# One-hot places by one comparison for eight token tiles, in both routed stages of a gated cross-attention kernel

## The chip, the cores and the metric

The kernel runs on one core of one Trainium2 chip. The metric is the device time of one launch in microseconds (us). A core has TensorE (PE, the matmuls; PEld are its weight loads), VectorE (DVE), ScalarE (ACT), GpSimd (POOL) and SyncE (SP), and DMA queues issued from several of them.

## The reference, cut to what matters

Four layers of cross-attention, each followed by a feed-forward part, work on 16 x 128 = 2048 tokens of width 256. Layers 0 and 2 have a mixture of experts as their feed-forward part (MoE 0 and MoE 2 below): a router gives each token two of eight experts, and every token also passes through a shared expert.

```python
logits = x @ gate_w.T
scores = jax.nn.softmax(logits, axis=-1)
topk_w, topk_idx = jax.lax.top_k(scores, K)          # K = 2 of E = 8
...
y_sel = y_all[topk_idx, tok]                          # y_all: silu(x w1) * (x w3) @ w2, of each expert
y = jnp.sum(y_sel * topk_w[..., None], axis=1)
shared = jax.nn.silu(x @ sw1) * (x @ sw3) @ sw2
return (y + shared).reshape(hidden_states.shape)
```

## The kernel before, in words

The tokens lie in SBUF as 16 tiles of 128 partitions (B = 16, P = 128). In a routed stage the kernel computes no expert for tokens that did not choose it. It sorts the 4096 pairs of token and expert into blocks of 128 rows, each block of a single expert: at most NBLK = 40 blocks. `spots` finds the position `ps` of each pair in that order, and splits it into a block `blk` (0 to 39) and a place `at` within the block (0 to 127). Then it builds the inverse, `who`: which token stands in each place of each block. POOL gathers the normalised tokens by `who` with indirect DMAs (`load`, L593 in MoE 0 and L848 in MoE 2, two for each pair of blocks), and the experts' matmuls run over the blocks.

The inverse is a product of one-hot matrices, summed over 32 tiles of pairs (2 choices x 16 token tiles). For tile q the matrix `inp[:, q]` (128 x 128) has a nonzero element where a token's place equals the column's number, and `inb[:, q]` (128 x 40) a one where its block equals the column's number; TensorE adds `inp[:, q].T @ inb[:, q]` into `w` (L436, 32 matmuls), so that `w[place, block]` is the token's number. Before the change the number stands in `inp`: each of 32 instructions (L431) compares the row `slot` (0 to 127) with the tile's place and multiplies by the tile's token numbers, both per-partition scalars. `inb` comes from one comparison of 1280 elements (L421). `inp` is made in four tiles of eight, from three buffers shared under the tag `xn`; the fourth waits until the first has been read by TensorE. Both are written as fp32r, fp32 bits for TensorE's faster pass.

`spots` is a generator, run by `route` in `stage_moe0` and `stage_moe2`. The order of PE, DVE and ACT instructions is written out by hand (`manual_schedule`): between its yields the stage puts pieces of the shared expert (`fill`), so that TensorE has work while DVE routes. After the tile n of `inp` is made, the stage yields; before tiles 0 and 2 of the matmuls it places a `fill`:

```python
for n in range(4):
    next(r)
    if n % 2 == 0:
        fill()
next(r, None)
```

So TensorE's order is: shared expert, matmuls of `inp` 0 and 1, shared expert, matmuls of `inp` 2 and 3, and then the shared expert's rest while the gathers run. While DVE is busy with routing, the shared expert uses ACT and POOL in place of DVE. In MoE 0 a piece goes TensorE `up` (L477), ACT `sil` (L485, L490), POOL `hid` (L491), TensorE `th` (L497), ACT `hT` (L499), TensorE `y` (L505), ACT `ysh` (L511), POOL addition to `x` (L512). In MoE 2 it goes TensorE `ub` (L875), ACT `sil` and `gcopy` (L883, L889), POOL `hid` (L890), TensorE `tg` (L897), ACT `hT` and `hcopy` (L902, L904), POOL `hT` (L905), TensorE `yb` (L913), ACT `ysh` (L940), POOL addition to `x` (L941). After `who` (L437) the pieces use DVE again. The program holds the four layers a second time for inputs that need another softmax; that half does not run here.

Of the kernel before, what the change touches and what calls it, by code (L numbers as in the profile page):

```python
# [10 lines left out]
F32 = mybir.dt.float32  # L11
# [3 lines left out]
ALU = mybir.AluOpType  # L15
# [3 lines left out]
P = 128  # L19
B = 16  # L20
# [11 lines left out]
NBLK = 40  # L32
# [23 lines left out]
def passage(ctx: ExitStack, tc: tile.TileContext, a: dict, out: bass.AP, inv, flag):  # L56
    nc = tc.nc
# [108 lines left out]
    def bc(ap, axis, n):  # L166

        u = ap.unsqueeze(axis)
        shape = list(u.shape)
        shape[axis] = n  # L170
        return u.to_broadcast(shape)
# [170 lines left out]
    def sorter(pool):  # L342

        I32 = mybir.dt.int32
        c = {}
        upper = pool.tile([P, P], BF16, name="upper")
        nc.gpsimd.memset(upper, 1.0)
        nc.gpsimd.affine_select(
            out=upper, in_=upper, pattern=[[1, P]], compare_op=ALU.is_gt, fill=0.0, base=0, channel_multiplier=-1
        )  # L350
        onesb = pool.tile([P, P], BF16, name="onesb")
        nc.gpsimd.memset(onesb, 1.0)
        c["upper"], c["onesb"] = upper, onesb

        def counting(name, n, step, by_row):
            t = pool.tile([P, n], I32, name=f"{name}i")
            nc.gpsimd.iota(t, pattern=[[step, n]], base=0, channel_multiplier=by_row)
            c[name] = pool.tile([P, n], F32, name=name)
            nc.gpsimd.tensor_copy(c[name], t)

        counting("token", B, P, 1)
        counting("block", NBLK, 1, 0)
        counting("slot", P, 1, 0)

        for name, shape in (("ct", [P, E, B]), ("ce", [P, B, E])):
            c[name] = pool.tile(shape, F32, name=name)
            nc.gpsimd.memset(c[name], 1.0)
            nc.gpsimd.memset(c[name][:, :, 0:1], 0.0)
        return c
# [17 lines left out]
    def spots(mr, mo, psa, cn, one, pos, who, offs, inb):  # L387

        f, g = "p t e -> p (t e)", "p e t -> p (e t)"
        mb = mr.tile([P, B, E], BF16, name="mb")  # L390
        nc.vector.tensor_tensor(mb, one[:, 0], one[:, 1], ALU.add)
        yield
        pc = psa.tile([P, 2, B, E], F32, name="pc", tag="a")
        for i, w in enumerate((cn["upper"], cn["onesb"])):
            nc.tensor.matmul(pc[:, i].rearrange(f), lhsT=w, rhs=mb.rearrange(f), start=True, stop=True)
        cnt = mr.tile([P, E, B], F32, name="cnt")
        nc.vector.tensor_copy(cnt, pc[:, 1].rearrange("p t e -> p e t"))
        run = mr.tile([P, E, B], F32, name="run")
        nc.vector.tensor_tensor_scan(run.rearrange(g), cn["ct"].rearrange(g), cnt.rearrange(g), 0.0, ALU.mult, ALU.add)
        nb = mr.tile([P, E], F32, name="nb")  # L400
        nc.vector.tensor_scalar(nb, run[:, :, B - 1], 1.0 / P, 0.49609375, ALU.mult, ALU.add)
        nc.vector.tensor_scalar(nb, nb, MAGIC, None, ALU.add)
        nc.vector.tensor_scalar(nb, nb, MAGIC, None, ALU.subtract)
        be = mr.tile([P, E], F32, name="be")
        nc.vector.tensor_tensor_scan(be, ones[:, 0:E], nb, 0.0, ALU.mult, ALU.add)
        nc.vector.tensor_tensor(nb, be, nb, ALU.subtract)
        nc.vector.tensor_tensor(run, run, cnt, ALU.subtract)
        nc.vector.scalar_tensor_tensor(run, bc(nb, 2, B), float(P), run, ALU.mult, ALU.add)
        at = mr.tile([P, B, E], F32, name="at")
        nc.vector.tensor_tensor(at, pc[:, 0], run.rearrange("p e t -> p t e"), ALU.add)  # L410
        ps = mr.tile([P, 2, B], F32, name="ps")
        nc.vector.tensor_tensor(one, one, bc(at, 1, 2), ALU.mult)
        nc.vector.tensor_reduce(ps, one, AX.X, ALU.add)

        blk = mr.tile([P, 2, B], F32, name="blk")
        nc.vector.tensor_scalar(blk, ps, 1.0 / P, -0.49609375, ALU.mult, ALU.add)
        nc.vector.tensor_scalar(blk, blk, MAGIC, None, ALU.add)
        nc.vector.tensor_scalar(blk, blk, MAGIC, None, ALU.subtract)
        at = mr.tile([P, 2, B], F32, name="place")
        nc.vector.scalar_tensor_tensor(at, blk, -float(P), ps, ALU.mult, ALU.add)  # L420
        nc.vector.tensor_tensor(  # L421
            inb, bc(blk.rearrange("p i t -> p (i t)"), 2, NBLK), bc(cn["block"], 1, 2 * B), ALU.is_equal
        )
        yield

        w = psa.tile([P, NBLK], F32, name="w", tag="a")
        for q in range(0, 2 * B, 8):
            inp = mo.tile([P, 8, P], F32R, name="inp", tag="xn", bufs=3)
            for n in range(8):
                i, t = divmod(q + n, B)  # L430
                nc.vector.tensor_scalar(  # L431
                    inp[:, n], cn["slot"], at[:, i, t : t + 1], cn["token"][:, t : t + 1], ALU.is_equal, ALU.mult
                )
            yield
            for n in range(8):
                nc.tensor.matmul(w, lhsT=inp[:, n], rhs=inb[:, q + n], start=(q + n == 0), stop=(q + n == 2 * B - 1))  # L436
        nc.vector.tensor_scalar(who, w, B * P - 1.0, None, ALU.min)  # L437
        nc.vector.tensor_copy(pos, ps)

        le = mr.tile([1, NBLK, E], F32, name="le")  # L440
        jf = mr.tile([1, NBLK], F32, name="jf")
        nc.vector.tensor_tensor(le, bc(be[0:1], 1, NBLK), bc(cn["block"][0:1], 2, E), ALU.is_le)
        nc.vector.tensor_reduce(jf, le, AX.X, ALU.add)
        nc.vector.tensor_scalar(jf, jf, E - 1.0, float(WE), ALU.min, ALU.mult)
        nc.vector.tensor_copy(offs, jf)
# [12 lines left out]
    def stage_moe0(we, s13, s2, gw, tgc, sh, pos, wgt, cn, xs, ys, work):  # L458
# [63 lines left out]
        with tc.tile_pool(name="mr", bufs=1) as mr, tc.tile_pool(name="mo", bufs=2) as mo, tc.tile_pool(  # L522
# [48 lines left out]
            def route():  # L571

                t3 = lambda n: mr.tile([P, B, E], F32, name=n)
                l, ex = t3("l"), t3("ex")
                nc.vector.tensor_copy(l, lg)
                mx = mr.tile([P, 2, B], F32, name="mx")
                nc.vector.tensor_reduce(mx[:, 0], l, AX.X, ALU.max)
                nc.vector.tensor_tensor(ex, l, bc(mx[:, 0], 2, E), ALU.subtract)
                nc.scalar.activation(ex, ex, AF.Exp)
                one = first_two(mr, cn, ex, mx, -2.0)  # L580
                yield from spots(mr, mo, psa, cn, one, pos, who, offs, inb)
                s = mr.tile([P, B], F32, name="s")
                nc.vector.tensor_tensor(s, mx[:, 0], mx[:, 1], ALU.add)
                nc.vector.reciprocal(s, s)
                nc.vector.tensor_scalar(s, s, tg[:, tgc : tgc + 1], None, ALU.mult)
                nc.vector.tensor_tensor(wgt, mx, bc(s, 1, 2), ALU.mult)
# [152 lines left out]
    def stage_moe2(kv1, we, gw, gb, tgc, pos, wgt, cn, xs, ys):  # L739
# [4 lines left out]
        with tc.tile_pool(name="mr", bufs=1) as mr, tc.tile_pool(name="mo", bufs=2) as mo, tc.tile_pool(  # L744
# [60 lines left out]
            def route():  # L805
# [33 lines left out]
                nc.vector.tensor_reduce(wgt, gate, AX.X, ALU.add)  # L839
                nc.vector.tensor_scalar(wgt, wgt, tg[:, tgc : tgc + 1], None, ALU.mult)  # L840
                yield from spots(mr, mo, psa, cn, one, pos, who, offs, inb)

            xbs, xbTs, regs, hids, hTs = {}, {}, {}, {}, {}
# [1095 lines left out]
    with tc.tile_pool(name="kv1", bufs=1) as kv1:  # L1939
# [6 lines left out]
        cn = sorter(kv1)  # L1946
# [118 lines left out]
```

## Time and profile before

| | |
|---|---|
| median of 4 runs | 1064.28 us (1062.79 to 1065.0) |
| the profiled execution, its own time | 1062.89 us |
| its span, first to last instruction | 1061.1 us |
| mean granted TensorE clock | 0.912 |
| DVE busy | 609.7 us (57%) |
| POOL busy | 341.5 us (32%) |
| L431, one-hots of places | 64 instructions, median 336 ns, longest 2242 ns |
| L421, one-hots of blocks | 2 instructions of 1280 elements, 1482 ns |
| L436, their product | 64 matmuls, median 266 ns |
| `spots` in MoE 0, L421 to `who` | 177.4 to 196.5 us |
| `spots` in MoE 2, L421 to `who` | 635.3 to 654.8 us |

All times inside the program count from the start of the span. A row of the timeline has start, length, engine, line, operation, written and read tiles, count, and in brackets the idle time of the engine before it and what ended it. A row of the groups has the shapes, the count, the busy time, the mean in ns, and the idle time before. "Granted clock" is the share of TensorE's full clock that the chip gave; in this trace it is 1.0 or 0.5, and it changes at steps of a grid of 3.41 us.

### The profile page before, as it was taken

Reading aid. Unit: us, or ns where it says so; the run is one execution under the profiler, and the core shown is the slowest. Engines: PE = TensorE matmul, PEld = TensorE weight load, DVE = VectorE, ACT = ScalarE, POOL = GpSimd, SP = SyncE. Lnnn points to the kernel's source line nnn. Section 1 sums busy time; section 2 is a strip of 40 time slices with the busy share of each in tenths; the row PEclk is TensorE's granted clock in tenths of the full one; section 3 lists DMA queues with packets and bytes.
Section 4 is the critical chain, followed back from the end, with each engine's and each line's share of the span. In section 5 each row is a group of like instructions: output and inputs, shape, how many; then the busy total and the mean of one; then the engine's idle time right before and its main releaser. Section 6 shows DMA issues by size and latency. Waiting matters only on the chain. (4 is left out here: it accounts for less than half of the span.)

```text
span 1061.1 us, 14892 instructions
## 1 busy us (share of the span) xinstructions
PE 897.7 (85%) x5212; PEld 597.2 (56%) x5212; DVE 609.7 (57%) x1537; ACT 457.6 (43%) x707; POOL 341.5 (32%) x389
## 2 busy tenths in 40 slices
PE   2899978999999987888865758898179999998796
PEld 1444456777778544455443657887145555555564
DVE  5988866322224566777688678544445565434342
ACT  1211023233322446676763243455268888881111
POOL 5765422544105324311011126650533433101000
PEclk9999988999999988999996558999569999998899
DMA  9100070133332107900000202452588887610000
GB/s 305 45 1 0 1 210 34 55 104 110 80 119 71 42 24 108 117 1 1 1 1 0 80 0 65 145 141 82 147 249 248 231 221 217 166 41 1 21 31 33
DMA packets 71401, 94.12 MB, mean 89 GB/s; under 512 B 9271, under 2 KB 63127, under 8 KB 69015
## 3 DMA queue, kind: packets, MB, share of 16 engines
q1 hardware_dynamic: 56952, 67.21, 21.5%
q0 software_dynamic: 14080, 23.78, 11.4%
q10 hardware_dynamic: 288, 2.10, 0.5%
q8 instruction: 45, 0.74, 0.3%
q14 instruction: 36, 0.29, 0.1%
HBM read 57.06 MB, written 33.55 MB: 85 GB/s over the span
## 5 line engine op out<-in xcount | busy, mean ns | idle before, releaser
L1667 ACT ACTIVATE pt<-s 128x1024 f32<-128x1024 f32 x128 | 127.4, 1024 | 25.9 <-PE s L1660 22.1
L709 POOL DMA_INDIRECT yc<-ys,pos x64 | 62.3, 973 | 124.3 <-DVE x L729 48.8
L297 PE MATMUL y<-kv,toep 128*128 128x512 f32 x192 | 86.7, 603 | 1.1 <-DVE toep L237 1.1
L289 POOL TENSOR_TENSOR kv<-ctxT 128x1024 f32<-128x1024 f32 x32 | 60.2, 1899 | 28.5 <-PE y L297 28.5
L1676 PE MATMUL av<-pt,v 128*32 128x256 f32 x1024 | 69.2, 388 | 0.1
L1660 PE MATMUL s<-qa,ka 64*128 64x256 f32 x512 | 64.7, 334 | 3.4 <-ACT pt L1667 2.7
L1660 PEld LDWEIGHTS s<-qa,ka 64*128 64x128 f32 x512 | 38.8, 188 | 41.3 <-issue 18.2
L297 PEld LDWEIGHTS y<-kv,toep 128*128 128x128 f32 x192 | 35.6, 192 | 43.2 <-issue 39.8
L1687 DVE COPY avs<-av 128x256 f32<-128x256 f32 x64 | 27.1, 423 | 55.8 <-PE av L1676 55.8
L593 POOL DMA_INDIRECT xb<-xs,who x40 | 38.1, 952 | 41.1 <-PE tb L605 33.0
L616 PE MATMUL ub<-L0we,xbT 128*128 x160 | 50.7, 460 | 0.2 <-ACT xbT L607 0.2
L913 PE MATMUL yb<-L2we,hT 88*128 (+1 forms) x224 | 41.5, 312 | 7.8 <-DVE hT L737 5.0
L302 DVE TENSOR_TENSOR pr<-y,qT 128x1024 f32<-128x1024 f32 x32 | 39.0, 1222 | 12.3 <-PE y L297 9.4
L848 POOL DMA_INDIRECT xb<-xs,who x40 | 38.0, 950 | 22.9 <-PE tb L860 14.0
L1567 POOL TENSOR_TENSOR hl<-f,hl 128x512 fp32r<-128x512 f32 x16 | 20.5, 1281 | 74.3 <-ACT hl L1566 74.3
L477 PE MATMUL up<-L0s,xT 128*128 128x352 f32 x128 | 43.2, 483 | 0.0
L913 PEld LDWEIGHTS yb<-L2we,hT 88*128 88x128 f32 x224 | 33.1, 201 | 14.9 <-DVE hT L737 10.7
L1086 PE MATMUL s<-qa,ka 18*128 18x512 f32 x128 | 36.5, 647 | 4.2 <-ACT follow L1380 4.2
L305 DVE TENSOR_REDUCE oT<-pr 128x128 f32<-128x1024 f32 x32 | 38.9, 1219 | 1.0
L1676 PEld LDWEIGHTS av<-pt,v 128*32 128x32 f32 x1024 | 26.9, 110 | 20.4 <-issue 0.7
L642 PE MATMUL yb<-L0we,hTb 88*128 x160 | 37.9, 379 | 0.0
L1089 ACT ACTIVATE pt<-s 128x1024 f32<-128x1024 f32 x32 | 32.3, 1023 | 10.3 <-PE s L1086 10.1
(384 smaller groups left out, 2028.2 us busy)
## 6 DMA issues: line engine op xcount, KB each, us to landing
scr<-hl SPq DMA_DIRECT2D x64, 256.0 KB, 3.2
ys<-ysb SPq DMA_DIRECT2D x40, 256.0 KB, 2.1
qa<-scr SPq DMA_DIRECT2D x32, 256.0 KB, 4.3
ka<-scr SPq DMA_DIRECT2D x32, 256.0 KB, 5.3
L2we<-in_L_w_dram POOLq DMA_DIRECT2D x6, 792.0 KB, 6.5
L0we<-in_L_w_dram SPq DMA_DIRECT2D x6, 704.0 KB, 7.5
xs<-xn SPq DMA_DIRECT2D x8, 512.0 KB, 4.0
ctxT<-in_ctxT_dram ACTq DMA_DIRECT2D x2, 1024.0 KB, 5.9
```

The costliest lines, as they stand in the source:

```text
L289: nc.gpsimd.tensor_tensor(t, bc(ch, 3, 8), bc(ch, 2, 8), ALU.mult)
L297: nc.tensor.matmul(y[:, ns], lhsT=T[:, h, d : d + P], rhs=kv[mc][:, ns], start=(mc == 0), stop=(mc == lc))
L302: nc.vector.tensor_tensor(pr, y.rearrange("p (b j i) -> p b j i", b=B, j=8), bc(qT[:, lc, :, hs], 2, 8), ALU.mult)
L305: nc.vector.tensor_reduce(oT[:, lc, :, hs], pr, AX.X, ALU.add)
L477: nc.tensor.matmul(t[:, n, 0 : 2 * I], lhsT=xT[:, c, b * P : (b + 1) * P], rhs=s13[:, c, n, :], start=(c == 0), stop=(c == 1),)
L593: nc.gpsimd.indirect_dma_start(out=xbs[s][:, i, :], out_offset=None, in_=xs, in_offset=bass.IndirectOffsetOnAxis(ap=who[:, 2 * s + i : 2 * ...
L616: nc.tensor.matmul(t[:, i, 0 : 2 * I], lhsT=xbT[:, i, c, :], rhs=we[:, bass.ds(regs[s][i] + c * 2 * I, 2 * I)], start=(c == 0), stop=(c == 1),
L709: nc.gpsimd.indirect_dma_start(out=got[b][:, i, :], out_offset=None, in_=ys, in_offset=bass.IndirectOffsetOnAxis(ap=pos[:, i, b : b + 1], ...
L913: nc.tensor.matmul(y[:, i, :], lhsT=hT[:, x, k, i, :], rhs=we[0:HI, bass.ds(at[i] + 4 * I + k * D, D)], start=(n == 0), stop=(n == 3),)
L1660: nc.tensor.matmul(s[:, h, jj, :], lhsT=ka[r, 2 * i + jj, sc * P : (sc + 1) * P], rhs=qa[r, 2 * i + jj, :], start=True, stop=True,)
L1667: nc.scalar.activation(pts[b, i][:, sc], s, AF.Exp)
L1676: nc.tensor.matmul(av[c : c + 32, :], lhsT=va[:, sc, 8 * h + 2 * i + jj, :], rhs=pt[:, sc, h, jj, :], start=(sc == 0), stop=(sc == 1),)
```

## The change

One-hots of eight token tiles are written by one comparison of 1024 elements, in which the places are broadcast along the columns and `slot` along the tiles. A comparison of that form cannot multiply by the token's number as well, so the number goes into the block rows: after L421, two instructions of 640 elements each multiply `inb` in place, one for each choice. `inp` then holds ones and `inb` token numbers; their product is the same `w`. In each routed stage 32 instructions become 4, and 2 are new. In the new file the products are L426, the comparison L433 and the matmuls L438.

```diff
         nc.vector.tensor_tensor(
             inb, bc(blk.rearrange("p i t -> p (i t)"), 2, NBLK), bc(cn["block"], 1, 2 * B), ALU.is_equal
         )
+        for i in range(2):
+            u = inb[:, i * B : (i + 1) * B]
+            nc.vector.tensor_tensor(u, u.bitcast(F32), bc(cn["token"], 2, NBLK), ALU.mult)
         yield
 
         w = psa.tile([P, NBLK], F32, name="w", tag="a")
         for q in range(0, 2 * B, 8):
             inp = mo.tile([P, 8, P], F32R, name="inp", tag="xn", bufs=3)
-            for n in range(8):
-                i, t = divmod(q + n, B)
-                nc.vector.tensor_scalar(
-                    inp[:, n], cn["slot"], at[:, i, t : t + 1], cn["token"][:, t : t + 1], ALU.is_equal, ALU.mult
-                )
+            i, t = divmod(q, B)
+            nc.vector.tensor_tensor(inp, bc(at[:, i, t : t + 8], 2, P), bc(cn["slot"], 1, 8), ALU.is_equal)
             yield
             for n in range(8):
                 nc.tensor.matmul(w, lhsT=inp[:, n], rhs=inb[:, q + n], start=(q + n == 0), stop=(q + n == 2 * B - 1))
```

`bc(ap, axis, n)` repeats a tile's values n times along a new axis, by a stride of zero.

## The prediction

> **What bounds the kernel now.** I read the page first, for the shares and the clock; then the timeline of both stretches in which `spots` runs; then the windows cut at the steps of the clock; last the waits of the second stretch and the groups by shape, for prices.
>
> ```profile
> PE 897.7 (85%) x5212; PEld 597.2 (56%) x5212; DVE 609.7 (57%) x1537; ACT 457.6 (43%) x707; POOL 341.5 (32%) x389
> ```
>
> TensorE is the busiest engine, and DVE work alone is worth nothing unless TensorE waits for it. The chain of waits reaches back to 739 us only, behind both routed stages, so I judge each stretch by its own timeline. In the first stage (MoE 0):
>
> ```profile
> 177.36 1.48 DVE L421 TENSOR_TENSOR inb<-blk,block 128x1280 fp32r<-128x1280 f32 x1
> 178.76 8.66 DVE L431 TENSOR_SCALAR inp<-slot,place,token 128x128 fp32r<-128x128 f32 x24
> ...
> 179.84 0.96 POOL L491 TENSOR_TENSOR hid<-sil 128x352 f32<-128x352 f32 x1 [3.14 <-issue]
> ...
> 180.85 0.55 PE L497 MATMUL th<-ident,hid 128*128 128x128 f32 x3 [0.75 <-POOL hid L491]
> ...
> 188.36 2.12 PE L436 MATMUL w<-inb,inp 128*128 128x40 f32 x16
> ...
> 189.63 2.75 DVE L431 TENSOR_SCALAR inp<-slot,place,token 128x128 fp32r<-128x128 f32 x8 [2.21 <-PE w L436]
> ...
> 196.30 0.20 DVE L437 TENSOR_SCALAR who<-w 128x40 uint32<-128x40 f32 x1 [3.92 <-PE w L436]
> ```
>
> The 24 one-hots end at 187.42, before TensorE reaches L436 at 188.36 behind the shared expert's matmuls; the last 8 end at 192.38, and TensorE takes them at 194.14. TensorE waits for POOL (`hid`, L491), never for `inp`. The second stage (MoE 2) is different:
>
> ```profile
> 635.30 1.48 DVE L421 TENSOR_TENSOR inb<-blk,block 128x1280 fp32r<-128x1280 f32 x1
> 635.31 2.26 POOL L890 TENSOR_TENSOR hid<-gcopy,sil 128x352 f32<-128x352 f32 x1 [0.62 <-ACT gcopy L889]
> ...
> 636.70 16.85 DVE L431 TENSOR_SCALAR inp<-slot,place,token 128x128 fp32r<-128x128 f32 x32
> ...
> 639.44 1.34 POOL L905 TENSOR_TENSOR hT<-hcopy,hT 88x512 fp32r<-88x512 f32 x1 [0.64 <-ACT hcopy L904]
> ...
> 646.39 1.42 PE L436 MATMUL w<-inb,inp 128*128 128x40 f32 x5 [1.60 <-DVE inp L431]
> ```
> ```profile
> 639.02:642.44 3.42, 2.25 (x18) 2.00 (x17) 3.42 (x7) 1.55 (x4) 2.24 (x2) 1.00 0.00 0
> 642.44:645.85 3.41, 2.35 (x19) 2.25 (x17) 3.41 (x4) 2.04 (x5) 3.05 (x3) 1.00 0.00 0
> 645.85:649.26 3.41, 2.87 (x12) 2.87 (x13) 3.41 (x13) 0.00 (x0) 0.40 (x1) 0.50 0.00 0
> 649.26:652.68 3.42, 3.42 (x15) 3.37 (x14) 3.42 (x8) 1.75 (x3) 2.11 (x2) 0.50 0.00 0
> 652.68:656.09 3.41, 3.41 (x31) 3.41 (x31) 2.30 (x7) 0.82 (x3) 2.47 (x3) 1.00 0.00 0
> ```
>
> Columns: length, busy time of PE, PEld, DVE, ACT, POOL, granted clock, DMA. Here TensorE waits 1.60 us for `inp`, and the clock is halved from 645.85 to 652.68: 2.87 + 3.42 = 6.3 us of work, about 3.1 us of it owed to the clock.
>
> **Durations.** One comparison repeats each 0.256 us (1.60 us for four, less one of 0.336, over three at 186 us), so eight cost 2.05 us undisturbed, and 32 cost 8.2 us per stage. For a `tensor_tensor` with both operands in SBUF there are two undisturbed rows:
>
> ```profile
> L421 DVE TENSOR_TENSOR inb<-blk,block 128x1280 fp32r<-128x1280 f32 x2 | 3.0, 1482 | 0.0
> L838 DVE TENSOR_TENSOR gate<-one,sq 128x256 f32<-128x256 f32 x1 | 0.4, 426 | 0.0
> ```
>
> That is (1482 - 426)/1024 = 1.03 ns an element, so 1024 elements take 1.22 us and 640 take 0.82 us. Consecutive instructions overlap by 0.08 us (L421 and L431 above: 177.36 + 1.48 - 178.76). L421 has the same two broadcast operands as the new comparison, so I see no reason for another rate.
>
> **Removed:** 64 comparisons, 8.2 us of DVE time in each stage. **Added** in each stage: two products, 2 x 0.74, and four comparisons, 4 x 1.14, net of overlap: 6.0 us. DVE thus gains some 2.2 us a stage if nothing disturbs it. The order on the other engines stands; only the first of eight matmuls of L436 now waits for DVE, and it waits for a whole tile of eight. The products stand ahead of the first comparison, 1.5 us of DVE time that was not there. The fourth `inp` still waits for the first to be read (three buffers).
>
> The Trainium skill, "VectorE: DVE Perf Modes" (The perf-mode tier table), has a rule against this change: a fp32 `tensor_scalar` from SBUF runs at twice the rate of a `tensor_tensor`. Taken alone, as an estimate with its 0.96 GHz clock, eight comparisons would go from 0.53 us to 1.07 us; the rows above, 2.05 against 1.22, include the cost of each instruction and go the other way.
>
> **What the longer instructions do to POOL.** L890 at 635.31 took 2.26 us; the same operation elsewhere takes 0.93 (its median). It began with L421 and ended 0.8 us after it: it was held for L421's whole length. Conversely L431, 0.336 us at the median, reached 2.24 us beside POOL's work. So these engines exclude each other, and what changes is the length for which POOL can be held: L431 held it for at most 0.1 us (L491 beside 24 of them: 0.96 and 1.02), a comparison of 1.22 us can hold it for 1.2.
>
> "SBUF — State Buffer" (Who interferes with whom) says the same of a Vector instruction with two SBUF inputs against a GpSimd instruction that reads SBUF; by its whole-instruction lock, each new comparison may cost POOL its full length, which is the upper bound that the row gives.
>
> **Stage 0, sum.** The products run from 178.8 to 180.35. `hid`, ready for POOL at 179.84, starts 0.5 us later, and `th` (L497) waits for it already: TensorE +0.5. The three comparisons follow, with POOL's two operations between them, to 185.6; the next `hid`, ready at 184.81 + 0.5, waits another 0.25. The fourth comparison begins when L436 frees a buffer, near 190.4, and holds the next `hid` by about 0.8; behind it lie 1.54 us of `y` (L505), so nearly nothing is added. Sum +0.75. From below: POOL slips in each time, 0. From above: it is held for a whole comparison once more, 1.2 + 0.5, so +1.7. I take 0.75, as the two collisions fall out of the order. The gathers behind `who` have 10 us of slack (issued from 196.79, read by TensorE at 208), so TensorE's lateness counts, and it goes on to the end.
>
> **Stage 2, sum.** L421 ends at 636.70 for DVE, POOL's `hid` goes first, to 637.57. DVE then needs 1.48 (products) and 1.14 (one comparison), and POOL interposes L941, L905 and L890, 1.27 + 1.33 + 0.93 = 3.53: the first `inp` stands at 637.57 + 2.62 + 3.53 = 643.7. TensorE came to it at 643.50. The second follows after another L941 (1.29): 643.7 + 1.29 + 1.14 = 646.2. TensorE therefore waits at the same place for the same 1.6 us, though then all eight matmuls can run, where before the last had to wait for a comparison at 647.03. With the clock as before this gives between -0.3 and +0.6 for `who`: POOL's L905 and L890, which before were done before 646.3, now come after the second comparison, to 648.5, and the halved matmuls of L436 (8 x 0.256 = 2.05) cover nearly all of that. I take +0.3. What follows, the shared expert's rest to 664.7 and twenty blocks at 93% TensorE, shifts along.
>
> Whole: 0.75 + 0.3 = +1.05. The profiled execution took 1062.89 (span 1061.1, 1.8 around it), 1.4 under the median of 1064.28; to the median, 1065.3. A difference of 0.2%, 2.1 us, is about what a measurement of this kernel can tell from no change.
>
> **Rivals.**
> 1. *Slower: POOL held in MoE 2 costs a window of clock.* If L905 is held by a product (1 us), TensorE's work between 639.02 and 642.44, 2.25 us in a window that kept its clock, falls to some 1.3; the windows from 372.8 and 956.5 us, with 1.3 us of TensorE work each, lost it. Then the 2.35 us up to 645.85 cost twice as much, about +1.7 in place of +0.3 by the order of L436 and the shared matmuls: +2.5 with stage 0. One more window at half rate, 652.68 to 656.09, adds up to 1.7: +4.2. It decides from about half a microsecond of POOL delay before 642.4. For it: L890's 2.26. Against: POOL's operations there have gaps of 0.6 and 1.1 us.
> 2. *Faster: `inp` is early enough.* If DVE gets through between POOL's operations, the second `inp` is there by 644.4, when TensorE has done the first eight (643.5 + 0.9), the 1.60 vanish, the window stays busy and the clock does not fall: -1.6 - 3.1, and +0.75 from stage 0: -4.0. For it: DVE's undisturbed sum, 636.7 + 1.5 + 2.3 = 640.5, is far ahead of 643.5. Against: 3.5 us of POOL work stand in the way.
> 3. *It does not do what it says:* the double broadcast or the in-place product is slower than 1.03 ns an element. At twice that, DVE needs 12 us against 8.2, the second stage's wait grows by about 2, and the whole is near +3. L421 speaks against it.
>
> **How the numbers follow.** The forecast, +1.05 and within 0.2%, gets 0.45. Slower by over 0.2% (rivals 1 and 3, 1066.8 to 1068.5) 0.35; faster by over 0.2% (rival 2, 1060.3, or less of it) 0.20. The range leaves out a tenth on either side: from 1060.8, near the whole of rival 2, to 1068.3, near the whole of rival 1. The likeliest case's own range is 1064.0 to 1066.4.
>
> **What would show it.** Right: 8 rows of the comparison at 1.2 us undisturbed, 4 products at 0.8; L491 in MoE 0 beginning or ending some 0.5 us late, L436 there at about 189.1; in MoE 2 a wait for the second `inp` still of 1 to 2 us. Wrong: no wait before L436 in MoE 2 and a full clock from 645.85 (rival 2); a halved clock from 642.44 (rival 1); a comparison over 1.4 us beside an idle POOL (rival 3).

## The result and the profile after

The changed kernel takes 1064.62 us (median of 42 runs), the kernel before 1064.73 (68 runs on the same chips); the ratio is 1.001 with a 95% interval of 1.0001 to 1.0019, so +0.1 to +2.0 us, with +1.1 in the middle. The medians hardly differ: the difference is a tail. Nine of the 44 recorded executions of the changed kernel (the median uses 42 of them) lie at 1070 to 1072.5 us, with a mean granted clock of 0.900 to 0.903, against 0.904 to 0.911 in the others; of the 68 before none is above 1069.5.

The page of the profiled execution (1067.94 us, span 1066.1; it lies towards that tail):

```profile
PE 904.3 (85%) x5212; PEld 601.6 (56%) x5212; DVE 600.8 (56%) x1485; ACT 457.8 (43%) x707; POOL 347.6 (33%) x389
```

DVE lost 52 instructions and 8.9 us of busy time, POOL gained 6.1 us with the same 389 instructions. The groups of the changed kernel (busy time, mean of one, idle time before):

```profile
L433 DVE TENSOR_TENSOR inp<-place,slot 128x1024 fp32r<-128x1024 f32 x8 | 14.6, 1870 | 4.9 <-PE w L436 4.9
L426 DVE TENSOR_TENSOR inb<-inb,token 128x640 fp32r<-128x640 f32 x4 | 4.8, 1242 | 0.1
```

L433's shortest took 1.212 us and L426's 0.820; the means, 1.87 and 1.24, hold the time in which they stood back for POOL. The timeline of MoE 0 after the change:

```profile
176.11 1.49 DVE L421 TENSOR_TENSOR inb<-blk,block 128x1280 fp32r<-128x1280 f32 x1
177.63 1.56 DVE L426 TENSOR_TENSOR inb<-inb,token 128x640 fp32r<-128x640 f32 x2
178.59 1.39 POOL L491 TENSOR_TENSOR hid<-sil 128x352 f32<-128x352 f32 x1 [3.14 <-issue]
179.11 4.76 DVE L433 TENSOR_TENSOR inp<-place,slot 128x1024 fp32r<-128x1024 f32 x3
180.03 0.55 PE L497 MATMUL th<-ident,hid 128*128 128x128 f32 x3 [1.19 <-POOL hid L491]
...
188.91 1.82 POOL L491 TENSOR_TENSOR hid<-sil 128x352 f32<-128x352 f32 x1 [3.30 <-issue]
189.42 1.54 PE L505 MATMUL y<-L0s,hT 128*128 128x256 f32 x6
190.80 0.54 PE L497 MATMUL th<-ident,hid 128*128 128x128 f32 x3
```

POOL's first `hid` is held by the second product, 1.39 against 0.96 before, and `th` waits 1.19 us for it where it waited 0.75. The last `hid`, 1.82, is held by the fourth comparison, but TensorE is at `y` until it is ready: `th` at 190.80 does not wait. In MoE 2:

```profile
636.89 1.49 DVE L421 TENSOR_TENSOR inb<-blk,block 128x1280 fp32r<-128x1280 f32 x1
636.90 2.26 POOL L890 TENSOR_TENSOR hid<-gcopy,sil 128x352 f32<-128x352 f32 x1 [0.62 <-ACT gcopy L889]
638.41 3.25 DVE L426 TENSOR_TENSOR inb<-inb,token 128x640 fp32r<-128x640 f32 x2
641.59 8.60 DVE L433 TENSOR_TENSOR inp<-place,slot 128x1024 fp32r<-128x1024 f32 x4
...
646.47 1.86 PE L436 MATMUL w<-inb,inp 128*128 128x40 f32 x16
646.86 2.24 POOL L905 TENSOR_TENSOR hT<-hcopy,hT 88x512 fp32r<-88x512 f32 x1
649.06 1.91 POOL L890 TENSOR_TENSOR hid<-gcopy,sil 128x352 f32<-128x352 f32 x1
649.15 1.38 PE L913 MATMUL yb<-L2we,hT 88*128 88x256 f32 x7 [0.62 <-POOL hT L905]
```

The first 16 matmuls run without the 1.60 us wait, and DVE is through with `inp` at 650.2. In its place TensorE waits for POOL, whose `hT` and `hid` took 2.24 and 1.91 us. From L421 to `who` its waits for POOL add up to 3.9 us, against 2.6 before, so 1.3 of the 1.60 saved came back. The windows of the clock (length, busy PE, PEld, DVE, ACT, POOL, granted clock, DMA):

```profile
639.53:642.94 3.41, 3.17 (x13) 2.78 (x11) 3.41 (x3) 1.58 (x4) 3.02 (x2) 0.50 0.02 5
642.94:646.36 3.42, 2.68 (x19) 2.48 (x20) 3.42 (x3) 1.96 (x4) 2.87 (x2) 1.00 0.00 0
646.36:649.77 3.41, 2.79 (x24) 2.59 (x23) 3.41 (x2) 0.90 (x3) 3.41 (x3) 1.00 0.00 0
649.77:653.18 3.41, 2.92 (x14) 2.58 (x13) 0.41 (x1) 1.73 (x3) 2.47 (x2) 0.50 0.00 0
653.18:656.60 3.42, 3.42 (x17) 3.42 (x16) 0.00 (x0) 0.83 (x3) 2.21 (x2) 0.50 0.00 0
```

The clock was full while the first 16 matmuls of L436 ran, and then halved for 13.65 us, to 663.42, against 6.83 us before; the window from 639.53 had been halved too.

### The profile page after: what moved, and what is told of

The parts are those of the page before. It is cut to its first block, busy times and chain, and to the rows that moved or that the text cites. A ratio compares the mean times of both kernels' runs of the same rounds, so it can differ in the third digit from the quotient of the medians.

```text
span 1066.1 us, 14840 instructions
## 1 busy us (share of the span) xinstructions
PE 904.3 (85%) x5212; PEld 601.6 (56%) x5212; DVE 600.8 (56%) x1485; ACT 457.8 (43%) x707; POOL 347.6 (33%) x389
## 5 line engine op out<-in xcount | busy, mean ns | idle before, releaser
L1667 ACT ACTIVATE pt<-s 128x1024 f32<-128x1024 f32 x128 | 127.4, 1024 | 26.5 <-PE s L1660 22.6
L1089 ACT ACTIVATE pt<-s 128x1024 f32<-128x1024 f32 x32 | 32.3, 1023 | 11.1 <-PE s L1086 10.9
```

The lines of the kernel that those rows point to most:

```text
L1667: nc.scalar.activation(pts[b, i][:, sc], s, AF.Exp)
```

## The experiments

Three explanations are told apart, called by letters in the expectations. Theory A: the long DVE instructions hold POOL, and TensorE waits for POOL. Rival B: the added or remaining work of DVE itself is the cost. Rival C: the whole difference is where the stage lies on the grid of the clock.

Two lengths carry the reading of all of them: from the start of L421 to TensorE's first transpose of gathered tokens (L605 in MoE 0, L860 in MoE 2). The third column is the time of halved clock within the second length. All are of one profiled execution each; lines below are the experiments' own.

| kernel | MoE 0, us | MoE 2, us | halved, us | time against before |
|---|---|---|---|---|
| before | 31.01 | 29.37 | 7.2 | |
| changed | 31.38 | 33.14 | 17.1 | 1.0010 (1.0001 to 1.0019) |
| e1, MoE 0 only | 31.38 | 28.59 | 6.8 | 1.0009 (0.9994 to 1.0023) |
| e2, MoE 2 only | 31.01 | 28.05 | 8.1 | 0.9991 (0.9979 to 1.0003) |
| e3, products alone | 31.36 | 28.11 | 6.8 | 0.9996 (0.9985 to 1.0007) |
| e4, operands in PSUM | 30.76 | 22.64 | 0 | 0.9937 (0.9918 to 0.9956) |
| e5, comparisons twice | 32.38 | 33.17 | 10.2 | 1.0041 (1.0021 to 1.0060) |
| e6, e4 and comparisons twice | 30.76 | 28.51 | 5.5 | 0.9973 (0.9952 to 0.9994) |
| e7, e4 with places in SBUF | 30.91 | 31.16 | 8.0 | 0.9970 (0.9945 to 0.9994) |
| e8, before with L421 from PSUM | 31.00 | 31.50 | 8.0 | 1.0003 (0.9981 to 1.0024) |
| e9, before, MoE 2 delayed | 31.01 | 29.95 | 13.7 | 1.0028 (1.0014 to 1.0042) |
| e10, changed, MoE 2 delayed | 31.40 | 30.19 | 17.1 | 1.0036 (1.0019 to 1.0052) |
| e11, e4, MoE 2 delayed | 30.75 | 24.03 | 3.6 | 0.9971 (0.9960 to 0.9983) |
| e12, e4 again | 30.76 | 23.93 | 0.2 | 0.9966 (0.9953 to 0.9979) |

MoE 0 runs at full clock throughout and repeats to 0.02 us; MoE 2 does not repeat, as the changed kernel, e2 and e10 show with the same MoE 2 code: 33.14, 28.05, 30.19. So each step of theory A is read from MoE 0, and MoE 2 tells, roughly, what it costs.

The two profiled executions, before and changed, warn against reading more from one profile. Their spans differ by 5.0 us, and 4.1 of it lies in the two lengths; but the unchanged stretch between the two stages is 2.5 us longer as well, and the unchanged part ahead of L421 in MoE 0 is 1.25 shorter. In MoE 2 the 9.9 us more at half clock can be worth up to 5 us (an estimate: half of them), while TensorE's waits there, 3.9 us in all against 4.2 before, did not grow. So by this estimate most of the 3.8 us is the clock's.

**e1 and e2: one stage at a time.** `spots` takes a flag, and the old loop or the new line runs.

```diff
-yield from spots(mr, mo, psa, cn, one, pos, who, offs, inb)
+yield from spots(mr, mo, psa, cn, one, pos, who, offs, inb, True)   # in the stage kept changed; False in the other
```

> The change in MoE 0 alone; MoE 2 is as before. Theory A (long DVE instructions hold POOL, and TensorE waits for POOL's hid): L421 to the end of the matmuls of L436 in MoE 0 lasts 0.4 to 0.8 us longer than before's 18.9, MoE 2 is unchanged, the time is before +0.4 to +0.8. Rival B (the two products ahead of the first comparison are the cost): no change in MoE 0, where the one-hots are not waited for, so before +0.0. Rival C (the whole difference is the phase of the clock's grid): no lengthening of MoE 0, time within 0.1% of before.

> The change in MoE 2 alone; MoE 0 is as before. Theory A: POOL's hid and hT (0.93 and 1.33 us undisturbed) show 1.3 to 2.3 us there, TensorE does not wait for inp any more but for POOL, and the clock is halved at some point between L421 and the gathers; time before +0 to +2.5 us. Rival B: the first matmul of L436 waits for inp by 1 us or more. Rival C: POOL's durations as before, time as before.

MoE 0 lengthened by 0.37 us, the same as in the changed kernel (0.38 to the end of L436, just under theory A's 0.4 to 0.8); B and C had zero. In e2 the operations of POOL that met the new instructions took 1.51 to 2.25 us, and nothing of TensorE waited for `inp`, as A had it; in e1, with the old MoE 2, the waits list has it still:

```profile
PE w L442 <- DVE inp L436: 1.9, 1, 1.9
```

The times alone, +0.09% and -0.09%, hold zero in both intervals; e2's leaves only the lower end of the 0 to 2.5 us that A expected.

**e3: the products alone.** The comparisons stay short and lose their multiplication.

```diff
-            i, t = divmod(q, B)
-            nc.vector.tensor_tensor(inp, bc(at[:, i, t : t + 8], 2, P), bc(cn["slot"], 1, 8), ALU.is_equal)
+            for n in range(8):
+                i, t = divmod(q + n, B)
+                nc.vector.tensor_scalar(inp[:, n], cn["slot"], at[:, i, t : t + 1], None, ALU.is_equal)
```

> The comparisons stay 32 instructions of 128 elements (without the multiplication), and the products into the block rows are added: the extra work alone, without the long comparisons. Theory A: POOL is held by the products only, once or twice by 0.8 us at most, and DVE ends later than before by 1.5 us: in MoE 2 the wait of TensorE for inp grows from 1.6 to about 3 us; before +1 to +2. Rival B: the same kernel time as the changed kernel plus the wait, before +1.5 or more, all of it in MoE 2. Rival C: as before.

MoE 0 is 31.36, so nearly all of its +0.37 comes with the products, of which the second holds one `hid` (1.38 us). A's longer wait for `inp` in MoE 2 did not come: TensorE paused once within L436, for 0.43 us. The time is that of before, as C had it; A's +1 to +2 and B's were both misses.

**e4: the same instructions, one operand in PSUM.** Places, block numbers and token numbers lie in columns of the PSUM tile `pc` that nothing used.

```diff
-        pc = psa.tile([P, 2, B, E], F32, name="pc", tag="a")
+        pcs = psa.tile([P, 2 * B * E + 5 * B], F32, name="pc", tag="a")
+        pc = pcs[:, 0 : 2 * B * E].rearrange("p (a t e) -> p a t e", a=2, t=B)
+        held = pcs[:, 2 * B * E : 2 * B * E + 4 * B].rearrange("p (a i t) -> p a i t", a=2, i=2)
+        tok = pcs[:, 2 * B * E + 4 * B :]
...
+        nc.vector.tensor_copy(tok, cn["token"])
...
-        nc.vector.tensor_scalar(blk, blk, MAGIC, None, ALU.subtract)
-        at = mr.tile([P, 2, B], F32, name="place")
+        nc.vector.tensor_scalar(held[:, 0], blk, MAGIC, None, ALU.subtract)
+        blk, at = held[:, 0], held[:, 1]
...
-            nc.vector.tensor_tensor(u, u.bitcast(F32), bc(cn["token"], 2, NBLK), ALU.mult)
+            nc.vector.tensor_tensor(u, u.bitcast(F32), bc(tok, 2, NBLK), ALU.mult)
```

> The changed kernel with the places, the block numbers and the token numbers held in PSUM, in unused columns of the tile pc, so that L421's comparison, the products and the new comparisons each read only one operand from SBUF; one copy of 16 elements per stage is added. Theory A: POOL is no longer held: hid in MoE 0 stays at 0.93 to 1.0 us, and hid and hT in MoE 2 at 0.93 and 1.33; DVE's comparisons are at 1.22 us each even beside POOL; the wait for inp in MoE 2 is gone; the time falls to 2 to 5 us below before, 3 to 6 below the changed kernel. Rival B: no gain over the changed kernel, as the same instructions run in the same order. Rival C: the same as before within 0.1%.

> The kernel with operands in PSUM, once more, beside the kernels with fills: the difference to the one with fills is the price of 1.7 us of delay and of half a window of phase. Theory A: 0.992 to 0.997 of before. Rival C: within 0.2% of before.

6.7 us below before in e4, 3.6 in e12 on another chip. DVE and POOL side by side in MoE 2, from e4's timeline:

```profile
637.94 1.28 POOL L909 TENSOR_TENSOR hT<-hcopy,hT 88x512 fp32r<-88x512 f32 x1
639.17 0.95 POOL L894 TENSOR_TENSOR hid<-gcopy,sil 128x352 f32<-128x352 f32 x1
641.22 1.28 POOL L945 TENSOR_TENSOR x<-x,ysh 128x512 f32<-128x512 f32 x1 [1.09 <-ACT ysh L944]
...
639.33 4.84 DVE L437 TENSOR_TENSOR inp<-pc,slot 128x1024 fp32r<-128x1024 f32 x4
```

Four comparisons take 4.84 us where they took 8.60, and POOL beside them is at its undisturbed length. TensorE has no gap left in the window from 642.49, and the clock holds from 632.3 to 734.7:

```profile
642.49:645.90 3.41, 3.41 (x29) 3.39 (x29) 1.54 (x2) 1.39 (x4) 2.31 (x4) 1.00 0.00 0
```

Rivals B and C fall: the same instructions in the same order, with one copy of 16 elements more, are 0.34% to 0.63% below before. No run moved the operands of the 32 short comparisons to PSUM, so how much of this the kernel before could have had without the long ones is not shown. The rule of the Trainium skill's page "SBUF — State Buffer" (Who interferes with whom), that a Vector instruction with a single SBUF input outside the two-port modes leaves GpSimd alone, agrees with these rows.

**e5 and e6: every comparison twice,** in the changed kernel and in e4's.

```diff
-            nc.vector.tensor_tensor(inp, bc(at[:, i, t : t + 8], 2, P), bc(cn["slot"], 1, 8), ALU.is_equal)
+            for _ in range(2):
+                nc.vector.tensor_tensor(inp, bc(at[:, i, t : t + 8], 2, P), bc(cn["slot"], 1, 8), ALU.is_equal)
```

> The changed kernel with every comparison of 1024 elements issued twice, into the same tile: 4.6 us more DVE work in each stage, all of it with two operands from SBUF. In MoE 0 the one-hots still come before TensorE reads them. Theory A (POOL is held by each such instruction): POOL's hid and hT meet twice as many of them; MoE 0 lengthens by a further 0.5 us or more, MoE 2 by 3 us or more, the time is 4 to 8 us above the changed kernel. Rival C (only the clock's phase): MoE 0 unchanged, MoE 2 longer only by a wait for inp, 0 to 3 us.

> The kernel with the operands in PSUM, every comparison issued twice: the same extra DVE work without the second operand from SBUF. Theory A: POOL's hid and hT stay at 0.93 and 1.28 us, MoE 0 is not lengthened, and MoE 2 only by what TensorE waits for inp: the first inp is ready near 641.7 + 0 to 1 in place of 640.5, the second near 644 against 642.7 when TensorE wants it, so a wait of 1 to 2 us; time 0 to 3 us above the kernel in PSUM, and still below before. Rival B (DVE's own work is the cost): as much above the PSUM kernel as the doubled SBUF kernel is above the changed one.

POOL's `hid` in MoE 0, from the groups of e5 and then of e6:

```profile
L492 POOL TENSOR_TENSOR hid<-sil 128x352 f32<-128x352 f32 x4 | 6.1, 1513 | 10.2 <-issue 10.2
```
```profile
L496 POOL TENSOR_TENSOR hid<-sil 128x352 f32<-128x352 f32 x4 | 3.7, 933 | 12.1 <-issue 12.1
```

From SBUF, the extra work lengthened MoE 0 by 1.0 us over the changed kernel; from PSUM by nothing. The whole, 0.31% or 3.3 us above the changed kernel's ratio, is a little under the 4 to 8 that A expected, and of the 3 us or more expected in MoE 2 the profile shows nothing: 33.17 against 33.14. Between the two, with equal DVE work, lies 0.68% of the time, 7 us. In MoE 2 the extra work costs e6 something as well, 28.51 against 22.64 and 23.93 for e4's kernel. The expected wait is not it, as TensorE waited 0.27 us for the second `inp` and not 1 to 2; the 5.5 us of halved clock are worth up to 2.8, and the rest stays open. By the times alone rival B would stand: doubling costs e4's kernel 0.07% (against e12) to 0.36% (against e4) and the changed one 0.31%. It is MoE 0, 1.0 us against nothing, that tells the two apart.

**e7 and e8: which instruction.** e7 is e4 with the places in SBUF; e8 is the kernel before with only the block numbers in PSUM (`held`, columns of `pc` as in e4).

```diff
# e7, against e4
-        blk, at = held[:, 0], held[:, 1]
+        blk = held[:, 0]
+        at = mr.tile([P, 2, B], F32, name="place")
# e8, against before
-        nc.vector.tensor_scalar(blk, blk, MAGIC, None, ALU.subtract)
+        nc.vector.tensor_scalar(held, blk, MAGIC, None, ALU.subtract)
+        blk = held
```

> The kernel in PSUM, but with the places in SBUF again: only the four comparisons read two operands from SBUF, L421 and the products one. Theory A: POOL's hid and hT are held by comparisons up to 2.3 us in MoE 2, and most of the gain of the PSUM kernel (6 us) is lost: time within 3 us of before. If instead L421 and the products were what held TensorE up, it keeps more than half of the gain, 1060 or less.

> The kernel before, with the block numbers in PSUM so that L421 alone no longer reads two operands from SBUF; its 32 short comparisons stay. Theory A: POOL's hid at L421 takes 0.93 us in place of 2.26, TensorE's wait for it shrinks by 1.3 us in MoE 2; the wait for inp stays, as the comparisons still stand back for POOL: 1 to 2.5 us below before. If L421 were the whole source of the gain of the PSUM kernel, 5 us or more below before.

On the chip of e5 to e8 the kernel before took 1077.46 us, so only ratios count. In e7 POOL was held in MoE 2 for 2.24 us (`hT`, L910) and 1.91 (`hid`, L895) by comparisons alone, and its time is 0.30% (3.2 us) under before, just outside what A expected. e4 was not run beside it, and e12's gain is 0.34%, so whether any of the gain was lost stays open; the profile does not help, as its MoE 2 lasted 31.16 us, longer than before. In e8's MoE 2 L421 met no `hid`, which had ended 0.6 us earlier, but the addition to `x` (L944): it took 1.29 us, its undisturbed length, so POOL was not held. The expected 1 to 2.5 us did not appear, though an interval of -0.19% to +0.24% leaves room for their smaller part.

**e9 to e11: half a window later.** Two fills of `inb`, 1.125 and 0.592 us on DVE, ahead of MoE 2's routing.

```diff
                 nc.vector.tensor_copy(l, lg[:, :, 1, :])
+                nc.vector.memset(inb.bitcast(F32), 0.0)
+                nc.vector.memset(inb[:, 0:B].bitcast(F32), 0.0)
```

> The kernel before with two fills of the block rows with zeros (1280 and 640 elements, about 1.7 us of DVE, overwritten later) ahead of MoE 2's routing, so that everything in MoE 2 stands half a window later against the clock's grid. If MoE 2's length depended on its own work alone, before +1.7 us. Theory A with the clock as its price: L421 to the first gather's transpose differs from the 28.6 and 29.4 us seen in two executions of the same MoE 2 by up to 3 us, and the time is between before +0 and +4.

> The changed kernel with the same two fills ahead of MoE 2's routing. Theory A with the clock as its price: POOL's hid and hT show 1.3 to 2.3 us whatever the phase, and the length from L421 to the first transpose lies between the 28.1 and 33.1 us seen so far; time 0 to 3 us above the kernel before with the fills. Rival C (nothing but phase): on this phase the two kernels can be in the other order, the changed one 1 us or more below.

> The kernel with operands in PSUM with the same two fills. Theory A: POOL's durations stay at 0.93 and 1.28 us at this phase too, and the length from L421 to the first transpose stays within 2 us of 22.6; it is 3 us or more below the kernel before with the fills. Rival C: the gain was a lucky phase, and the time is within 2 us of the kernel before with the fills.

1.7 us of delay cost the kernel before 1.5 to 4.5 us and the changed kernel about as much (1.0036 against 1.0010); which of the two is ahead at this phase the intervals do not tell. POOL was held in e10 much as A had it, 1.51 to 2.39 us. e4's kernel stays 0.57% below before with the same delay (0.9971 against 1.0028), so its gain does not hang on one phase.

## Why the prediction was right, and where it was not

- **The forecast** of +1.05 us, within 0.2%, was measured as +1.1. That the two agree so closely is luck. The median did not move, the +1.1 is the tail of nine long executions, and neither stage did what its term says.
- **Durations** were right: comparisons 1.212 us at least (1.22 forecast), products 0.82 (0.82). Rival 3 falls with it. The working given for the short comparisons' 0.256 us is not: 1.60 less 0.336, over three, is 0.42, as one of those four was held. The figure itself stands by a row of the kernel before, 15 of them in 3.92 us from 646.77.
- **MoE 0: +0.37, not +0.75.** The first collision was right, 0.45 us for 0.5, and so was the third, hidden behind `y`. The mis-sized term is the second, 0.25 us, which was zero: the three comparisons were to end 8.24 us after L421's start (185.6), 0.3 after the `hid` was ready, and they ended 7.75 after it, at 183.86, before the `hid` of 183.98. With POOL's addition between the first and the second of them (1.71 us, most of it waiting), the work after the first `hid` took 3.9 us where I had 4.3.
- **MoE 2: the wait for `inp` was to stay at 1.6 us; it vanished.** The failed step is "POOL interposes L941, L905 and L890": DVE and POOL took turns, and only L941 and L905 came ahead of the first comparison. The first `inp` came 7.0 us after L421's start and the second 8.9, where I had 8.4 and 10.9. Most of what was saved, 1.3 us, came back as waits for POOL, whose operations took up to 2.24 us; I had that price, but in rival 1. The stage was neither the forecast nor one rival: early `inp` from rival 2, held POOL from rival 1.
- **The clock** was taken to stay as before. In the profiled execution it was halved for 17.1 us of MoE 2 instead of 7.2, and MoE 2 was 3.8 us longer; in e2 8.1 us and 1.3 us shorter. Rival 1's price, +2.5 to +4.2, is about the 4.1 us by which the two stages were longer in that execution. The nine long runs lie further out, 5.5 to 7.8 us above the median, and none of them was profiled; that they are this case at its worst is argued, not shown.
- **The 2:1 rule** quoted in the prediction, for `tensor_scalar` against `tensor_tensor`, did not decide: eight short comparisons took 2.05 us undisturbed, one long one 1.21.

Open: why the clock falls in one execution and not in another of the same code. TensorE's busy time in a window does not sort it: at full clock 2.35 us (before, from 642.44) and 2.79 (changed, from 646.36) were followed by a halved window, 2.25 (before, from 639.02) was not. The executions also enter MoE 2 differently. A long halved stretch ahead of it lasted 58.03 us in before and changed, and 54.61 in e1 and e2, where the clock was back 3.8 and 3.9 us ahead of L421, and not within 1 us of it. In the first pair the changed MoE 2 is 3.8 us longer than the old one, in the second 0.5 shorter (28.05 against e1's 28.59). With one execution of each this is an observation and no cause. e4's kernel is short after either stretch: 22.64 after 54.61 us, 23.93 in e12 after 58.03.

With executions of the same MoE 2 code at 28.05, 30.19 and 33.14 us, and an interval of -0.2% to 0 for e2, the sign of the change's effect in MoE 2 is not settled; what is shown is that POOL is held and that TensorE then waits for POOL.

## What to carry to other kernels

Before merging many short DVE instructions into a few long ones, look at what GpSimd does beside them: the longer instruction finishes DVE's work sooner, but if it reads two operands from SBUF it can hold a GpSimd operation for its whole length, and the engine that waits for GpSimd pays. Put one operand into PSUM where a column is free: here that turned a change without a gain into one of 3.6 to 6.7 us. And where executions of the same code differ in how long TensorE's clock is halved, compare many runs, not one profile.

## What the runs showed of the hardware that was not expected

- DVE and POOL, both with operands in SBUF, mostly took turns when DVE's instructions were long. In the changed kernel L433 and L905, L890, L941 alternated through MoE 2, each lasting its own length and part or all of the other's (L433 1.94 to 2.31 us, POOL 1.35 to 2.24). That is no rule: in e2 and e7 one long comparison lasted 3.18 and 3.06 us, behind two POOL operations in a row, as a short one did before (L431 at 2.24 us).
- The same code of MoE 2 ran 5 us apart in two executions (33.14 and 28.05 us from L421 to L860), with 9 us more at half clock. L421 began 0.8 us and 0.5 us behind a step of the grid, but the clock had come back one step earlier in the short one, and POOL's `hid`, which began together with L421 in the long one, was already done.
